# Two-layer graph network: the first layer norm on ScalarE, the own-feature products made ahead, and row chunk 0's own tiles kept for hop 1

## The chip, the cores and the metric

The kernel runs on one core of a Trainium2 chip. A core has five engines that work side by side, each through its own list of instructions in order: TensorE (PE in the profile) multiplies matrices into PSUM; VectorE (DVE), ScalarE (ACT) and GpSimd (POOL) do element-wise work; SyncE (SP) here only issues DMAs. ScalarE can issue DMAs too, between its other instructions. All DMAs run on sixteen DMA engines. Engines wait for each other through semaphores. The metric is the device time of one execution in microseconds (us); lower is better.

## What is computed

There are 4096 nodes with 64 features each and a sparse 4096 x 4096 matrix `adj` (64 MB in fp32). Layer 0 normalises the features, clips them at zero, and makes two hops; each hop multiplies by `adj`, puts the product beside the features it came from, and multiplies by a 128 x 64 weight. Layer 1 normalises again and sums neighbours with weights that are powers of a half, by the neighbour's rank in its row.

```python
h = relu(layernorm(x))
for k in range(2):                       # two hops
    agg = adj @ h
    h = tanh(concatenate([agg, h], axis=1) @ W[k])
x = x + h
h = relu(layernorm(x))
support = h @ weight
rank = cumsum(adj != 0, axis=1)
deg = rank[:, -1:]
k = minimum(deg, 100.)
pos = rank - (deg - k)
w = (adj != 0) * where(pos > 0, 0.5 ** (k - pos), 0.0)
x = x + (w @ support + bias)
```

`concatenate([agg, h]) @ W[k]` is two products added: the aggregate with the upper half of `W[k]`, and the node's own features with the lower half. The second is called the own-feature product here.

## The kernel before, in words

**Tiles.** `adj` is cut into four row chunks I = 0..3 of 1024 rows and 32 column blocks b of 128 columns. Transposed, one tile (I, b) is 128 x 1024 fp32, 512 KB. A feature tensor is held as 32 blocks of 128 nodes: `hx[:, b, :64]` holds the normalised features, `hx[:, b, 64:]` the result of hop 0. One matmul multiplies 64 or 128 columns of `hx` (the weights of TensorE) with 512 columns of a tile.

**Sweep 1** (`sweep1`) goes through the row chunks in order and, in each, through sixteen pairs of column blocks from b = 31 down to 0. For a pair n it issues the two loads on SP, then `count_pair` on DVE (five instructions that make the running count of non-zeros and store it as bytes in `codes`), then the matmuls of hop 0, then one `step()`, which carries a queue of small jobs written as generators on by one `yield`. A pair whose blocks lie in a row chunk that is already finished is *fused*: its matmul takes all 128 columns of `hx`, so that hop 1 is done for that tile in the same pass (L317). The other tiles (L211) get hop 0 alone and are loaded a second time in sweep 2.

**Buffers.** The pairs rotate through `ring` (three pairs) and, for I < 3, through the part of `codes` that belongs to row chunk 3 (four pairs more), so seven pairs can be loaded ahead. A pair's slot comes free when both DVE has counted it and TensorE has multiplied it.

**The first layer norm** (`ln_relu`) runs in row chunk 0, a chunk of eight blocks at a time: chunk 3 before the second pair, chunks 2, 1 and 0 as small jobs put in at n = 1, 5 and 9. Each has four wide instructions and one small one on DVE, a square on ACT, and a power of -0.5 on POOL (L157). The pairs n = 4q to 4q + 3 need chunk 3 - q. `load_x` and `load_weights` issue the loads of x and of the weights on SP, the weights between the first pair's loads and the second's.

**Finishing a row chunk.** `features_T` (at n = 12 of each row) transposes the chunk's own features into `hT`. `finish_row` then copies the sums out (`S`, `F`, and `tot`, the row counts, which waits for the last count), multiplies them and `hT` by the weights into `po`, takes the tanh (`x1T`), transposes it back into `hx[:, :, 64:]`, keeps hop 1's own part in `pre1`, and turns `tot` into `base` on DVE from the PSUM tile `pb`. Its parts are spread over the first pairs of the next row.

**Sweep 2** (`sweep2`) loads the tiles that were not fused again for hop 1, in the order of `parts`, and puts layer 1 between: `decode` turns codes into powers of two (ACT and DVE, L406, L398, L401), `add_base` adds `base` on DVE (L416), `layer1` multiplies. `share` says how many units of layer 1 go with each pair of tiles.

Of the kernel before, what the change touches and what calls it, by code (L numbers as in the profile page):

```python
# [7 lines left out]
F32 = mybir.dt.float32  # L8
# [8 lines left out]
P = 128  # L17
# [14 lines left out]
def gnn_kernel(  # L32
# [63 lines left out]
    def tmp(shape=None, dtype=F32, name="tmp"):  # L96
        return tpool.tile(shape or [P, C], dtype, tag="tmp", name=name)
# [4 lines left out]
    def two(name="two"):  # L102
        return pone.tile([P, C], F32, tag="two", name=name)


    def load_x(q):
        nc.sync.dma_start(pre1[:, chunk(q), :], xv[:, chunk(q), :])

# [5 lines left out]
    def load_weights():  # L114
        for h in range(2):
            rows = slice(h * D, (h + 1) * D)
            for k in range(HOPS):
                nc.sync.dma_start(wz[rows, h, k], W[k].rearrange("(h d) e -> d h e", h=2))
            nc.sync.dma_start(wa[rows], weight)

    warm = spool.tile([P, 1], F32, tag="warm", name="warm")
    nc.vector.memset(warm, 0.0)
# [20 lines left out]


    def ln_relu(dst, src, scale=1.0):
        wide = lambda ap: ap[:, :, None].to_broadcast([P, CB, D])
        s1 = spool.tile([P, CB], F32, tag="s1", name="s1")
        s2 = spool.tile([P, CB], F32, tag="s2", name="s2")
        xc = tmp([P, CB, D], name="xc")
        sq = tmp([P, CB, D], name="sq")  # L150
        nc.vector.tensor_reduce(s1, src, axis=AX.X, op=ALU.add)
        nc.vector.scalar_tensor_tensor(xc, wide(s1), -1.0 / D, src, op0=ALU.mult, op1=ALU.add)
        nc.scalar.activation(sq, xc, AF.Square)
        yield
        nc.vector.tensor_reduce(s2, sq, axis=AX.X, op=ALU.add)
        nc.vector.tensor_scalar(s2, s2, 1.0 / D, EPS, op0=ALU.mult, op1=ALU.add)  # L156
        nc.gpsimd.tensor_tensor(s2, s2, half, op=ALU.pow)  # L157
# [4 lines left out]
        nc.vector.scalar_tensor_tensor(dst, xc, 0.0, wide(s2), op0=ALU.max, op1=ALU.mult)  # L162
        return dst


    by_t = lambda ap: ap.rearrange("q (p t) -> q t p", t=TC)
# [70 lines left out]
        nc.scalar.copy(by_t(hT), pt.rearrange("q (t p) -> q t p", t=TC))  # L237
        return hT

    def finish_row(I, acc, hT):  # L240
        S = tmp(name="S")
        nc.scalar.copy(S, acc[:, NC, :])
        if I:
            F = [tmp(name="F") for _ in range(NC)]
            for c in range(NC):
                nc.scalar.copy(F[c], acc[:, c, :])
        tot = tmp([P, CW], BF16, name="tot")
        nc.scalar.copy(
            tot.rearrange("p (k m) -> p k m", k=2),
            cnts[I % 2].bitcast(U8).rearrange("p (m k) -> p k m", k=2),  # L250
        )
        yield
        po = one(name="po")
        terms = [(lambda c: wz[:, c, 0, 1], lambda c: hT), (lambda c: wz[:, c, 0, 0], lambda c: S)]
        if I:
            terms.append((lambda c: wz[:, 0, 0, 0], lambda c: F[c]))
        paired(po, terms)
        terms = [(lambda c: wz[:, 1, 1, 0], lambda c: F[c])] if I else []
        po1 = two(name="po1")
        if I:  # L260
            for c in range(NC):
                nc.tensor.matmul(
                    po1[c * D : (c + 1) * D, :], wz[:, 1, 1, 0], F[c], start=True, stop=False
                )
        x1T = tmp(name="x1T")
        nc.scalar.activation(x1T, po, AF.Tanh)
        yield
        pt = nodes(x1T)
        for c in range(NC):
            nc.tensor.matmul(  # L270
                po1[c * D : (c + 1) * D, :], wz[:, c, 1, 1], x1T, start=I == 0, stop=True
            )
        nc.scalar.copy(as_nodes(hx[:, chunk(I), D:]), pt)
        nc.scalar.copy(flat(pre1[:, chunk(I), :]), po1)
        yield
        for c in range(NC):
            pb = (one if c else two)(name="pb")
            nc.tensor.matmul(pb, tri, tot[:, c * C : (c + 1) * C], start=True, stop=True)
            nc.vector.tensor_scalar(
                base[:, I * CW + c * C : I * CW + (c + 1) * C], pb,  # L280
                off, -32768.0, op0=ALU.add, op1=ALU.max,
            )

    def sweep1():
        seq = 0
        first = ln_relu(hx[:, chunk(NCH - 1), :D], pre1[:, chunk(NCH - 1), :])
        load_x(NCH - 1)
        for I in range(NCH):
            acc = pacc.tile([P, 3, C], F32, tag="acc", name="acc")
            slots = [ring[:, s : s + 2, :] for s in range(0, RING, 2)]  # L290
            if I < NCH - 1:
                slots += [ring2[:, s : s + 2, :] for s in range(0, ring2.shape[1], 2)]
            for n, b in enumerate(range(NB - 1, 0, -2)):
                a = slots[seq % len(slots)]
                seq += 1
                for r in range(2):
                    nc.sync.dma_start(a[:, r, :], adjA[I, b - r])
                if I == 0:
                    if n == 0:
                        load_weights()  # L300
                        next(first)
                    elif n == 1:
                        for q in range(NCH - 2, -1, -1):
                            load_x(q)
                count_pair(I, b, a)
                if I == 0:
                    if n == 0:
                        for _ in first:
                            pass
                    if n % 4 == 1 and n < 12:  # L310
                        q = NCH - 2 - n // 4
                        steps.append(ln_relu(hx[:, chunk(q), :D], pre1[:, chunk(q), :]))
                for r in range(2):
                    g = b - r
                    if fused(I, g):
                        for c in range(NC):
                            nc.tensor.matmul(  # L317
                                acc[:, c, :], hx[:, g, :], a[:, r, c * C : (c + 1) * C],
                                start=g == CB * I - 1, stop=g == 0,
                            )  # L320
                    else:
                        agg_pair(acc[:, NC, :], hx[:, g, :D], a[:, r], g == NB - 1, g == CB * I)
                step()
                if n == 12:
                    hT = features_T(I)
            steps.append(finish_row(I, acc, hT))
            step()


# [176 lines left out]
    def sweep2():  # L506
        n_ring = 4
        early = pacc.tile([P, 3, C], F32, tag="acc", name="acc1")
        accs = {2: early[:, 0, :], 3: early[:, 1, :]}
        parts = [(2, 16, 24), (3, 24, 32), (2, 24, 32), (1, 8, 32), (0, 0, 32)]  # L510

        share = [0, 0, 0, 16 / 12, 22 / 16]
        owed = 0.0
        seq = 0
        space(ring[:, 4, :].bitcast(I16).rearrange("p (r k m) -> p r k m", r=2, k=2))
        space(ring[:, 5, :].bitcast(I16).rearrange("p (r k m) -> p r k m", r=2, k=2))
        for i, (I, b0, b1) in enumerate(parts):
# [63 lines left out]
```

## Time and profile before

| what | value |
|---|---|
| median of 3 runs | 478.34 us (475.04 to 479.42) |
| the profiled execution | 472.14 us, its span 470.1 us, 4623 instructions |
| busy in the span | PE 390.2 us, DVE 325.9 us, ACT 124.0 us, POOL 24.4 us |
| mean granted clock of TensorE | 0.956 |
| moved by DMA | 112.72 MB, mean 240 GB/s |

The profile is of one execution. A page gives busy times by engine, the span in forty slices, the DMA queues, the chain of work that ended last (followed back from the last instruction to what released it), and groups of instructions by source line. A group's row reads: line, engine, operation, output<-inputs, shape, xcount | busy us, mean ns of one | idle time of the engine just before, and what ended it. TensorE works an fp32 matmul in two passes, each with a record of its own, so a count of records is twice the count of matmuls; records of the two column halves overlap. By stages the span reads: sweep 1's row chunk 0 until about 64 us, row chunk 1 until 110, row chunks 2 and 3 until 211, sweep 2 until about 392, and the rest of layer 1 until 470.

### The profile page before, as it was taken

How to read it: one execution, taken by the hardware profiler on the slowest of the kernel's cores; microseconds unless marked ns; L12 is line 12 of the kernel's file. 1: busy time of each engine (PE TensorE's matmuls, PEld its weight loads, DVE VectorE, ACT ScalarE, POOL GpSimd, SP SyncE). 2: the span in 40 equal slices, each digit the busy share in tenths (PEclk: the TensorE clock that was granted, in tenths of full speed). 3: DMA queues.
4: the chain of work that ended last, by engine and by line, in shares of the span. 5: the costliest groups of instructions: out<-in, count | busy, mean ns of one | idle time of the engine just before them, and what ended most of it. 6: DMA issues, size and time to landing. Idle time of an engine off the chain costs nothing.

```text
span 470.1 us, 4623 instructions
## 1 busy us (share of the span) xinstructions
PE 390.2 (83%) x1632; PEld 147.1 (31%) x1632; DVE 325.9 (69%) x548; ACT 124.0 (26%) x150; POOL 24.4 (5%) x17
## 2 busy tenths in 40 slices
PE   0766599999999999996867958789879998953995
PEld 0211243344344434442212412223323333311342
DVE  4799998999999779750104564444688998997332
ACT  1000020012000300004001325353476775582000
POOL 0212200000000000000002030000110000200000
PEclk9997899999999999999999888899899999977999
DMA  7999999999987488837899654566457880000011
GB/s 213 371 410 408 410 401 366 379 388 393 348 313 261 162 282 316 299 117 270 312 337 322 227 180 162 196 229 241 160 199 252 279 293 5 1 1 0 1 45 45
DMA packets 32742, 112.72 MB, mean 240 GB/s; under 512 B 4560, under 2 KB 4560, under 8 KB 32720
## 3 DMA queue, kind: packets, MB, share of 16 engines
q1 hardware_dynamic: 32720, 112.44, 66.4%
q8 instruction: 12, 0.20, 0.2%
q14 instruction: 10, 0.08, 0.1%
HBM read 111.38 MB, written 1.05 MB: 239 GB/s over the span
## 4 chain that ended last, share of the span: by engine, by line
PE 53%; DVE 28%; DMA 9%; ACT 4%; issue 3%; POOL 2%; SPq 1%; ACTq 0%; POOLq 0%; DVEq 0%
PE acc L317 15%; PE acc L211 15%; PE accl L448 9%; DMA ring<-in_adjA_dram 9%; DVE m L194 5%; DVE ring L416 5%; PE accl L457 5%; DVE codes L204 4%; DVE codes L416 3%; PE pt L181 3%; PE po L172 2%; DVE codes L471 2%; ACT ring L406 2%; DVE lo L205 2%; POOL s L157 2%
## 5 line engine op out<-in xcount | busy, mean ns | idle before, releaser
L211 PE MATMUL acc<-ring,hx 128*64 128x512 f32 x472 | 118.5, 627 | 33.3 <-DVE hx L162 21.2
L211 PEld LDWEIGHTS acc<-ring,hx 128*64 128x64 f32 x472 | 33.2, 145 | 99.0 <-issue 41.2
L317 PE MATMUL acc<-ring,hx 128*128 128x512 f32 x144 | 63.0, 595 | 0.0
L416 DVE TENSOR_TENSOR ring<-ring,base 128x2048 uint16<-128x2048 int16 x34 | 41.1, 1219 | 29.3 <-ACT ring L406 29.3
L448 PE MATMUL accl<-ring,hx 128*128 128x512 bf16 x136 | 38.7, 412 | 25.4 <-DVE ring L416 18.3
L204 DVE TENSOR_TENSOR codes<-m,lo 128x512 uint16<-128x512 uint16 x124 | 52.8, 426 | 4.2
L194 DVE TENSOR_SCALAR m<-ring 128x2048 uint8<-128x2048 f32 x37 | 45.2, 1221 | 5.4 <-DMA ring<-in_adjA_dram 5.4
L448 PEld LDWEIGHTS <-hx 128*128 128x128 bf16 x256 | 23.5, 102 | 81.1 <-issue 47.2
L406 ACT ACTIVATE ring<-codes 128x1024 int16<-128x1024 uint8 x44 | 43.6, 1047 | 17.8 <-PE accl L457 17.8
L211 PE MATMUL acc<-codes,hx 128*64 128x512 f32 x168 | 39.9, 614 | 7.4 <-DVE hx L162 7.4
L406 ACT ACTIVATE codes<-codes 128x1024 int16<-128x1024 uint8 x42 | 40.7, 1042 | 12.0 <-PE accl L457 12.0
L205 DVE TENSOR_SCALAR lo<-codes 128x512 uint16<-128x512 uint16 x128 | 37.6, 294 | 4.5
L317 PEld LDWEIGHTS acc<-ring,hx 128*128 128x128 f32 x144 | 27.0, 190 | 34.5 <-issue 34.5
L157 POOL TENSOR_TENSOR s<-s,half 128x8 f32<-128x8 f32 x8 | 17.1, 2141 | 386.9 <-DVE s L156 386.9
L416 DVE TENSOR_TENSOR codes<-codes,base 128x2048 uint16<-128x2048 int16 x30 | 35.5, 1217 | 0.8 <-ACT codes L406 0.8
L448 PE MATMUL accl<-codes,hx 128*128 128x512 bf16 x120 | 30.3, 389 | 5.1 <-ACT codes L406 5.1
L194 DVE TENSOR_SCALAR m<-codes 128x2048 uint8<-128x2048 f32 x27 | 33.0, 1221 | 0.0
L237 ACT COPY hT<-ph 128x512 f32<-128x512 f32 x4 | 4.4, 1106 | 97.1 <-PE ph L232 97.1
L457 PE MATMUL accl<-ring,lo 128*64 128x512 bf16 x136 | 22.2, 428 | 0.0
L211 PEld LDWEIGHTS acc<-codes,hx 128*64 128x64 f32 x168 | 11.9, 141 | 32.2 <-issue 21.3
L317 PE MATMUL acc<-codes,hx 128*128 128x512 f32 x48 | 21.3, 597 | 0.0
L471 DVE TENSOR_TENSOR codes<-accl,codes 128x512 f32<-128x512 f32 x24 | 15.1, 683 | 7.2 <-PE accl L457 7.2
(74 smaller groups left out, 254.1 us busy)
## 6 DMA issues: line engine op xcount, KB each, us to landing
ring<-in_adjA_dram SPq DMA_DIRECT2D x154, 512.0 KB, 4.7
codes<-in_adjA_dram SPq DMA_DIRECT2D x54, 512.0 KB, 6.1
pre<-in_x_dram SPq DMA_DIRECT2D x4, 256.0 KB, 6.3
xres<-in_x_dram SPq DMA_DIRECT2D x4, 256.0 KB, 5.3
out_dram<-o SPq DMA_DIRECT2D x4, 256.0 KB, 2.5
wz<-in_W_dram SPq DMA_DIRECT2D x4, 32.0 KB, 5.4
wa<-in_weight_dram SPq DMA_DIRECT2D x2, 16.0 KB, 4.6
wz<-in_weight_dram SPq DMA_DIRECT2D x2, 16.0 KB, 4.4
```

The source lines that it names most:

```text
L157: nc.gpsimd.tensor_tensor(s2, s2, half, op=ALU.pow)
L181: nc.tensor.matmul(pt[:, t * P : (t + 1) * P], by_t(src)[:, t, :], ident, start=True, stop=True, skip_group_check=True,)
L194: nc.vector.tensor_scalar(m, a, 0.0, float(FLAG - 1), op0=ALU.not_equal, op1=ALU.mult)
L204: nc.vector.tensor_tensor(q, m[:, r].bitcast(U16), cnt, op=ALU.add)
L205: nc.vector.tensor_scalar(cnt, q, 0x7F7F, None, op0=ALU.bitwise_and)
L211: nc.tensor.matmul(acc[c * D : (c + 1) * D, :], src, a[:, c * C : (c + 1) * C], start=first, stop=last,)
L317: nc.tensor.matmul(acc[:, c, :], hx[:, g, :], a[:, r, c * C : (c + 1) * C], start=g == CB * I - 1, stop=g == 0,)
L406: nc.scalar.activation(w[:, r], src[:, r].rearrange("p (m k) -> p k m", k=2), AF.Copy, scale=float(FLAG))
L416: nc.vector.tensor_tensor(w.bitcast(U16), w, base[:, None, g * CW : (g + 1) * CW].to_broadcast([P, 2, CW]), op=ALU.add)
L448: nc.tensor.matmul(accs[-1][:, c, :], hm[:, CB * J + 2 * k + r, : 2 * D], w[:, r, c, :], start=k == 0 and r == 0, stop=k == CB // 2 - 1 an ...
L457: nc.tensor.matmul(acc[c * D : (c + 1) * D, 2, :], lo[:, CB * J + 2 * k + r, :], w[:, r, c, :], start=k == 0 and r == 0, stop=k == CB // 2 ...
L471: nc.vector.tensor_tensor(p, acc[:, q, :], p, op=ALU.add)
```

## The change

It has five parts, all in sweep 1 and in what sweep 2 takes over from it.

1. **Loads.** SP loads only two blocks of x (30 and 31) before the first pair; the other x loads and all weight loads are issued on ScalarE.
2. **Layer norm.** `ln_relu` is used for blocks 30 and 31 alone and finished before the first count. All other blocks use the new `ln_relu_blocks`: for each block two activations with a sum as second output (mean, then sum of squares), three POOL instructions on 128 x 8 values for the whole chunk, and one activation a block for the result.
3. **Own-feature products.** The new `own_share` makes the transposed features and their product with the lower half of `W[0]` for all four row chunks during row chunk 0 and keeps it in `pre1`; `finish_row` adds it on DVE ahead of the tanh.
4. **Kept tiles.** The last four pairs of row chunk 0 (blocks 7 to 0, the chunk's own columns) stay in their slots until the chunk's hop 0 is finished; hop 1 is then made from them, in a new part of `finish_row` (`agg_pair` over `held`), and `base` comes one part later.
5. **Sweep 2.** The part for row chunk 0 starts at block 8 rather than 0: eight loads and their matmuls fewer; its share of layer 1 is 22 units in 12 pairs rather than in 16.

```diff
-    def load_x(q):
-        nc.sync.dma_start(pre1[:, chunk(q), :], xv[:, chunk(q), :])
+    def load_x(engine, b0, b1):
+        engine.dma_start(pre1[:, b0:b1, :], xv[:, b0:b1, :])
...
-                nc.sync.dma_start(wz[rows, h, k], W[k].rearrange("(h d) e -> d h e", h=2))
-            nc.sync.dma_start(wa[rows], weight)
+                nc.scalar.dma_start(wz[rows, h, k], W[k].rearrange("(h d) e -> d h e", h=2))
+            nc.scalar.dma_start(wa[rows], weight)
...
+    def ln_relu_blocks(b0, b1):
+
+        nb = b1 - b0
+        m = spool.tile([P, CB], F32, tag="m", name="m")
+        s = spool.tile([P, CB], F32, tag="s", name="s")
+        junk = tmp([P, D], name="junk")
+        col = lambda ap, i: ap[:, i : i + 1]
+        for i in range(nb):
+            nc.scalar.activation(
+                junk, pre1[:, b0 + i, :], AF.Copy, scale=-1.0 / D, accum_out=col(m, i)
+            )
+            nc.scalar.activation(
+                junk, pre1[:, b0 + i, :], AF.Square, bias=col(m, i), accum_out=col(s, i)
+            )
+        s, m = s[:, :nb], m[:, :nb]
+        nc.gpsimd.tensor_scalar(s, s, 1.0 / D, EPS, op0=ALU.mult, op1=ALU.add)
+        nc.gpsimd.tensor_tensor(s, s, half[:, :nb], op=ALU.pow)
+        nc.gpsimd.tensor_tensor(m, m, s, op=ALU.mult)
+        yield
+        for i in range(nb):
+            nc.scalar.activation(
+                hx[:, b0 + i, :D], pre1[:, b0 + i, :], AF.Relu, scale=col(s, i), bias=col(m, i)
+            )
...
+    def own_share(I):
+
+        hT = features_T(I)
+        yield
+        po = two(name="po0")
+        paired(po, [(lambda c: wz[:, c, 0, 1], lambda c: hT)])
+        nc.scalar.copy(flat(pre1[:, chunk(I), :]), po)
+
...
-        terms = [(lambda c: wz[:, c, 0, 1], lambda c: hT), (lambda c: wz[:, c, 0, 0], lambda c: S)]
+        terms = [(lambda c: wz[:, c, 0, 0], lambda c: S)]
...
-        nc.scalar.activation(x1T, po, AF.Tanh)
+        nc.vector.tensor_add(x1T, po, flat(pre1[:, chunk(I), :]))
+        nc.scalar.activation(x1T, x1T, AF.Tanh)
...
         nc.scalar.copy(as_nodes(hx[:, chunk(I), D:]), pt)
+        yield
+        if I == 0:
+
+            for n, (b, a) in enumerate(held):
+                agg_pair(acc[:, 0, :], hx[:, b, D:], a, n == 0, n == len(held) - 1)
+            G = tmp(name="G")
+            nc.scalar.copy(G, acc[:, 0, :])
+            yield
+            for c in range(NC):
+                nc.tensor.matmul(
+                    po1[c * D : (c + 1) * D, :], wz[:, c, 1, 0], G, start=False, stop=True
+                )
         nc.scalar.copy(flat(pre1[:, chunk(I), :]), po1)
...
+                if I == 0 and n == 0:
+                    load_x(nc.scalar, NB - CB, b0)
+                    for _ in first:
+                        pass
+                    for q in range(NCH - 2, -1, -1):
+                        load_x(nc.scalar, q * CB, q * CB + CB)
+                    load_weights()
+                    for _ in ln_relu_blocks(NB - CB, b0):
+                        pass
+                if I == 0 and n % 4 == 1 and n < 12:
+                    q = NCH - 2 - n // 4
+                    steps.append(ln_relu_blocks(q * CB, q * CB + CB))
+                if I == 0 and n in (2, 6, 10, 13):
+                    steps.append(own_share(NCH - 1 - n // 4))
                 count_pair(I, b, a)
...
+                    if I == 0 and g < CB:
+                        held.append((g, a[:, r]))
                 step()
-                if n == 12:
-                    hT = features_T(I)
-            steps.append(finish_row(I, acc, hT))
+            steps.append(finish_row(I, acc, held))
...
-        parts = [(2, 16, 24), (3, 24, 32), (2, 24, 32), (1, 8, 32), (0, 0, 32)]
-
-        share = [0, 0, 0, 16 / 12, 22 / 16]
+        parts = [(2, 16, 24), (3, 24, 32), (2, 24, 32), (1, 8, 32), (0, 8, 32)]
+
+        share = [0, 0, 0, 16 / 12, 22 / 12]
...
-                agg_pair(acc, hx[:, b, D:], a, b == CB * I, b == NB - 1)
+                agg_pair(acc, hx[:, b, D:], a, b == max(CB * I, CB), b == NB - 1)
```

More of the change, by code (lines that the diff above doesn't have):

```diff
@@ L145, in ln_relu @@
     def ln_relu(dst, src, scale=1.0):
[L146 to L150, printed above, removed]
+        nb = src.shape[1]
+        wide = lambda ap: ap[:, :, None].to_broadcast([P, nb, D])
+        s1 = spool.tile([P, CB], F32, tag="s1", name="s1")[:, :nb]
+        s2 = spool.tile([P, CB], F32, tag="s2", name="s2")[:, :nb]
+        xc = tmp([P, CB, D], name="xc")[:, :nb]
+        sq = tmp([P, CB, D], name="sq")[:, :nb]
         nc.vector.tensor_reduce(s1, src, axis=AX.X, op=ALU.add)
@@ L156, in ln_relu @@
         nc.vector.tensor_scalar(s2, s2, 1.0 / D, EPS, op0=ALU.mult, op1=ALU.add)
-        nc.gpsimd.tensor_tensor(s2, s2, half, op=ALU.pow)
+        nc.gpsimd.tensor_tensor(s2, s2, half[:, :nb], op=ALU.pow)
         yield
@@ L238, in features_T, with finish_row @@
         return hT
-    def finish_row(I, acc, hT):
+    def own_share(I):
[4 more added lines that the diff above has]
+        nc.scalar.copy(flat(pre1[:, chunk(I), :]), po)
+    def finish_row(I, acc, held):
         S = tmp(name="S")
@@ L257, in finish_row @@
         paired(po, terms)
-        terms = [(lambda c: wz[:, 1, 1, 0], lambda c: F[c])] if I else []
         po1 = two(name="po1")
@@ L270, in finish_row @@
             nc.tensor.matmul(
-                po1[c * D : (c + 1) * D, :], wz[:, c, 1, 1], x1T, start=I == 0, stop=True
+                po1[c * D : (c + 1) * D, :], wz[:, c, 1, 1], x1T, start=I == 0, stop=I > 0
             )
         nc.scalar.copy(as_nodes(hx[:, chunk(I), D:]), pt)
+        yield
[9 more added lines that the diff above has]
+                )
         nc.scalar.copy(flat(pre1[:, chunk(I), :]), po1)
@@ L285, in sweep1 @@
         seq = 0
-        first = ln_relu(hx[:, chunk(NCH - 1), :D], pre1[:, chunk(NCH - 1), :])
-        load_x(NCH - 1)
+        b0 = NB - 2
+        load_x(nc.sync, b0, NB)
+        first = ln_relu(hx[:, b0:, :D], pre1[:, b0:, :])
+        held = []
         for I in range(NCH):
@@ L297, in sweep1 @@
                     nc.sync.dma_start(a[:, r, :], adjA[I, b - r])
[L298 to L304, printed above, removed]
-                count_pair(I, b, a)
[L306 to L312, printed above, removed]
+                if I == 0 and n == 0:
[12 more added lines that the diff above has]
+                    steps.append(own_share(NCH - 1 - n // 4))
+                count_pair(I, b, a)
                 for r in range(2):
```

## The prediction

> **What bounds the kernel now.** I read the span by stages first: busy time of each engine in three stretches (columns: stretch, length, then PE, PEld, DVE, ACT, POOL busy with instruction counts, granted clock, DMA share, GB/s).
>
> ```profile
> 14.40:64.40 50.00, 35.77 (x152) 11.62 (x154) 47.05 (x92) 3.59 (x5) 7.89 (x3) 0.90 1.02 407
> 64.40:110.00 45.60, 45.60 (x188) 17.74 (x186) 42.48 (x83) 5.50 (x9) 0.00 (x0) 1.00 1.00 383
> 110.00:211.00 101.00, 100.67 (x322) 43.07 (x318) 86.01 (x166) 9.17 (x13) 0.00 (x0) 1.00 0.76 273
> ```
>
> Row chunk 0 is paced by DVE (47 of 50 us busy) with the DMA engines full beside it (407 GB/s), while ACT works 3.6 us. Row chunk 1 is paced by DVE too: counting a pair takes 1.22 + 2 x (0.43 + 0.29) us plus gaps, 2.71 us from pair to pair in the timeline, and 16 x 2.71 = 43.4. Row chunks 2 and 3 are TensorE's (100.67 of 101.00). Next the timeline of row chunk 0, to see whom TensorE waits for:
>
> ```profile
> 22.66 2.68 POOL L157 TENSOR_TENSOR s<-s,half 128x8 f32<-128x8 f32 x1 [8.91 <-DVE s L156]
> ...
> 25.37 0.69 DVE L162 SCALAR_TENSOR_TENSOR hx<-xc,s 128x512 f32<-128x512 f32 x1
> ...
> 26.12 5.37 PE L211 MATMUL acc<-codes,hx 128*64 128x512 f32 x24 [2.29 <-DVE hx L162]
> ...
> 39.85 5.14 PE L211 MATMUL acc<-ring,hx 128*64 128x512 f32 x16 [6.65 <-DVE hx L162]
> ...
> 53.59 3.39 PE L211 MATMUL acc<-codes,hx 128*64 128x512 f32 x8 [5.15 <-DVE hx L162]
> ```
>
> The number in brackets is idle time and what ended it. TensorE needs 1.72 us for a pair (eight records, two side by side every 0.43 us) and is early each time; the chunk of normalised features releases it, at 26.1, 39.9 and 53.6, 13.8 us apart. The copy of the finished sum shows when row 0 is done on TensorE, and the rows of ACT and POOL give prices:
>
> ```profile
> 63.11 0.58 ACT L242 COPY S<-acc 128x512 f32<-128x512 f32 x1 [4.09 <-PE acc L211]
> ```
>
> ```profile
> L153 ACT ACTIVATE sq<-xc 128x512 f32<-128x512 f32 x8 | 5.0, 630 | 56.1 <-DVE xc L152 56.1
> ...
> L237 ACT COPY hT<-ph 128x512 f32<-128x512 f32 x4 | 4.4, 1106 | 97.1 <-PE ph L232 97.1
> ...
> L123 ACT ACTIVATE warm<-warm 128x1 f32<-128x1 f32 x1 | 0.2, 203 | 0.0
> ```
>
> So row 0 ends on TensorE at E = 63.0 us; row 1 is paced by DVE until 110; then nothing but TensorE's work counts until 211. An end of row 0 that comes later or earlier is passed on whole.
>
> **What the Trainium skill says.** *ScalarE: Activation LUTs*, What ACT_TABLE_LOAD costs: an ACTIVATE takes 186 ns + 0.833 ns an element with immediate scale and bias, 93 ns more for each per-partition pointer operand, and back-to-back ones overlap by 93 ns. The trace is near: 203 ns for one element, 630 for 512 (613 to 706 by the page). *SBUF — State Buffer*, Who interferes with whom: a DVE instruction with two SBUF inputs contends with a POOL instruction that reads SBUF. The trace agrees: L157 takes 1.65 us where DVE is waiting for it (12.10 us) and 2.61 to 2.68 beside counting. *VectorE: DVE Perf Modes*, Two Vector instructions with no wait between them: an operation that also writes its accumulator is two instructions; it says so of Vector, and no page prices it on ScalarE. *DMA: Bandwidth & Descriptors*, Issuing engines are not separate DMA queues: issuing from another engine saves only issue time. With 407 GB/s from SP alone, ACT's loads cannot add rate.
>
> **The change, part by part.** DVE is relieved: three chunks x (0.68 + 0.69 + 0.68 + 0.17 + 0.69) = 8.7 us, and 2 more at the start. Counting alone, from about 8 us, would be done at 8 + 43.4 = 51.4 instead of 64.4. But TensorE now waits for a chain over ACT and POOL, which I add up.
>
> *Start on ACT.* Ten DMAs move onto ACT's queue (SP's rows: 0.43 an x load, 0.7 a weight load). In the order of the changed kernel DMAs take eight completion semaphores in turn, and a DMA that reuses one waits until the earlier DMA on it has landed. So the last weight load waits on ACT for the first half of pair 3. Ahead of that stand 1.05 MB of x and seven halves, 4.7 MB; at 407 GB/s 11.6 us, after about 2 us to the first bytes, plus its own 0.7: A = 14.3 us. Behind it, in order, stands the first statistic. Bounds 11 to 17. SP gains the weight loads' 4.2 us, which nothing waits for any more.
>
> *One chunk on ACT.* Per block: Copy with a sum 0.24 us, Square with pointer bias 0.33 (the page's prices at 64 elements), each waiting for the one before (0.04 twice). The sum's read-out has no row: zero if it is free, 0.20 if it is an instruction like the 203 ns one; I take half, 0.10 twice. Total 0.85 a block, bounds 0.5 and 1.1; eight blocks 6.8, six 5.1. POOL: the power 2.65, and two small instructions that the trace does not show, between the 0.1 of a memset and the 1.3 of L363 on 128x512; I take 0.35 each and 0.15 for hand-overs: 3.5, bounds 2.5 and 5. Nothing on ACT can go ahead meanwhile. Results: 0.425 with two pointers less the overlap, 0.33 a block: 2.7 for eight, 2.0 for six.
>
> *Own products in the same queue.* Behind the results stand the copy hT (1.1), then the product on TensorE (four records, 0.86, and hand-overs: 1.0), then its copy (0.6 + 0.1), and only then the next chunk's first statistic. They are no extra work for ACT, but they are in the loop: 6.8 + 3.5 + 2.7 + 1.1 + 1.0 + 0.7 = 15.8 us per chunk, against 13.8 before.
>
> *End of row 0.* Six blocks: 14.3 + 5.1 + 3.5 + 2.0 = 24.9. Two loops: 56.5. Last chunk with its product: 15.1, 71.6. Then pairs 12 and 13 (3.4), the transposes (0.9), pair 14 (1.7), the product (0.9), pair 15 (1.7): E = 80.2, **17.2 us later**. Slots hold DVE back meanwhile, so that its relief is lost.
>
> *Row 1.* Four of seven pair slots stay held until hop 1. From E: pair 0 of row 1 and `po` 2.6; the new add on DVE 0.7 and tanh 0.6, pair 1, transposes and product until E + 7.4; pair 2; hop 1 is sixteen matmuls, 6.9, from E + 9.1. The first slot is released at E + 10.9, and a ring load lands 4.7 us after issue (the median): DVE, out of tiles, resumes at E + 15.5, counts two pairs, waits for `pb`, and has 11 x 2.71 left after E + 22.4: row 1 counted at E + 52.2. The add for row 1 stands behind one more count on DVE (2.7) and ahead of tanh, so TensorE's transposes begin at E + 56.3; before, 111.58 - 63.0 = 48.6. **Cost 7.7**; bounds 3 and 10.
>
> *Rows 2 and 3.* TensorE loses two sets of transposes (1.02 each) and one product (0.86): **-2.9**. The add hides behind a pair's 1.72 us there, since DVE is ahead.
>
> *Sweep 2.* Four pairs x 1.72 = 6.9 us of TensorE go. Around them DVE becomes the limit: from 345 to 390 it is busy 39.1 of 45 us and waits about 5 for TensorE. **-5**, bounds 0 and -8. The 4.2 MB fewer loads count nothing: no wait for DMA stands in that part.
>
> Sum: 17.2 + 7.7 - 2.9 - 5.0 = +17.0 us. On the profiled execution 472.14 + 17.0 = 489.1; that execution lies 6.2 below the median, to which I add it: 478.34 + 17.0 = 495.3.
>
> **The rivals.** *Faster: DVE's relief is what counts.* For it: DVE and DMA are the busy ones, ACT has 46 idle us in row 0. If the ACT loop were about 9 us, E would be DVE's 51.4 + 2.6 = 54, 9 us earlier: -9.0 + 7.7 - 2.9 - 5.0 = -9.2, 469 us. It decides below E = 63.2, a loop of about 11.4; 1% faster needs about 10. Against it: sixteen small instructions and one power alone give over 7.
> *Even: the low prices hold.* No read-out, 0.5 a block, POOL 2.5, results 0.27 a block: loop 11.5, E = 14.3 + 7.1 + 23 + 10.8 + 8.6 = 63.8, total +0.6: 479.
> *Dearer: every read-out 0.2 and POOL 4.2.* Loop 18.3, E about 90, total +27: 505.
> *The held slots do not stall* (loads land sooner): the forecast less 5, 490, inside its own range.
>
> **How the numbers follow.** Forecast 0.60, its own range 484 to 503; dearer 0.16; even 0.13; faster 0.11. The range 477 to 509 leaves out faster and a part of the even and dearer cases. About 1% (4.8 us) is what a measurement can tell from no change, the runs of before spreading 0.9%. Faster 0.11, within 1% 0.13, slower 0.76.
>
> **What would show it.** Right: TensorE idle in row 0 released by ACT's results, about 16 us apart; the row-0 sum copied near 80; ACT's first statistic near 14; a DVE wait for ring DMA of several us after hop 1. Wrong: the row-0 sum copied before 63, statistics under 0.55 a block, or DVE busy nine tenths up to 50 us.

## The result and the profile after

| | before | after |
|---|---|---|
| median on the same chip | 476.69 us (475.01 to 479.42) | 520.05 us (518.25 to 521.87) |
| ratio | | 1.0904, 95% interval [1.0825, 1.0983] |
| span of the profiled execution | 470.1 us | 516.5 us |
| mean granted clock of TensorE | 0.956 | 0.917 |
| moved by DMA | 112.72 MB | 108.55 MB |

The kernel became 9% slower: the direction was forecast, the size was not (495 forecast, range 477 to 509). Some executions of a kernel fall into a slower state, over 1.5% above its fastest; the ratios here leave them out, the medians do not. I cut both spans at marks that the trace shows in both kernels: the copy `S` of row 0's sum on ACT, and the first transpose (`pt`) on TensorE of the tanh of row 1, of row 3, and of the last two row chunks of sweep 2. Each column is the time from the mark before; the forecast is that of the prediction.

| us | to row 0's copy | to `pt` of row 1 | to `pt` of row 3 | to `pt`, second last of sweep 2 | to `pt`, last | to the end |
|---|---|---|---|---|---|---|
| before | 63.1 | 48.5 | 110.7 | 107.7 | 67.8 | 72.3 |
| after | 89.1 | 58.9 | 105.9 | 107.7 | 72.6 | 82.2 |
| difference | +26.0 | +10.4 | -4.8 | 0 | +4.8 | +9.9 |
| forecast | +17.2 | +7.7 | -2.9 | -5.0 from here on | | |

The differences add up to 46.3 of the 46.4 us. Each column is read from one execution. The fourth, where the code is all but the same in every kernel here, lies between 106 and 112 us in the experiments below, so that a difference of several us in it, or in the third, need not come from the code; the last two repeat within 1.5 us where the code there is the same. The busy time by stretch, for after (same columns as before: stretch, length, busy time of PE, PEld, DVE, ACT, POOL with counts, granted clock, DMA share, GB/s):

```profile
17.80:89.00 71.20, 42.13 (x202) 15.01 (x204) 37.03 (x71) 40.22 (x158) 13.45 (x12) 0.74 0.60 221
89.00:141.90 52.90, 49.38 (x186) 16.60 (x182) 41.26 (x79) 3.93 (x6) 0.00 (x0) 1.00 0.81 315
141.90:245.00 103.10, 102.32 (x309) 43.12 (x308) 86.40 (x166) 9.32 (x16) 0.00 (x0) 1.00 0.81 301
```

In row 0 no engine is full any more: TensorE, DVE and ACT are each busy for about half of it, the sign of one chain that passes through all of them, and the DMA engines fell from 407 to 221 GB/s. The timeline of ACT in row 0, which answers to the waits of TensorE shown of before:

```profile
17.86 0.26 ACT L174 ACTIVATE junk<-pre 128x64 f32<-128x64 f32 x1 [13.40 <-DMA wa<-in_weight_dram]
18.02 0.19 ACT L174 ACTIVATION_READ_ACCUMULATOR junk<-pre 128x1 f32 x1
18.24 0.35 ACT L177 ACTIVATE junk<-pre,m 128x64 f32<-128x64 f32 x1
18.50 0.19 ACT L177 ACTIVATION_READ_ACCUMULATOR junk<-pre,m 128x1 f32 x1
...
55.43 2.77 ACT L186 ACTIVATE hx<-pre,m,s 128x64 f32<-128x64 f32 x8 [3.99 <-POOL m L183]
58.10 1.06 ACT L262 COPY hT<-ph 128x512 f32<-128x512 f32 x1
61.24 0.59 ACT L271 COPY pre<-po 128x512 f32<-128x512 f32 x1 [2.08 <-PE po L197]
...
89.09 0.59 ACT L275 COPY S<-acc 128x512 f32<-128x512 f32 x1 [1.07 <-PE acc L236]
```

This is the loop of the prediction: statistics, a wait of 3.99 us for POOL, eight results, the copy `hT`, a wait of 2.08 us for the product, its copy, and only then the next chunk's first statistic. The copies of the products come at 44.12, 61.24 and 78.42: a loop is 17.1 to 17.2 us. TensorE shows the same loop from its side, and what it does to its pace:

```profile
42.08 1.97 PE L197 MATMUL po<-hT,wz 128*64 128x512 f32 x4 [4.27 <-ACT hT L262]
59.21 1.98 PE L197 MATMUL po<-hT,wz 128*64 128x512 f32 x4 [6.96 <-ACT hT L262]
...
76.41 1.97 PE L197 MATMUL po<-hT,wz 128*64 128x512 f32 x4 [7.05 <-ACT hT L262]
78.17 5.71 PE L236 MATMUL acc<-codes,hx 128*64 128x512 f32 x16
...
86.30 1.02 PE L197 MATMUL po<-hT,wz 128*64 128x512 f32 x4
```

The same four records take 1.97 us after an idle time of 4 to 7 us and 1.02 at 86.30, when TensorE has been busy for 8 us. The Trainium skill, *TensorE: Matmul & The Clock Gate*, Part 1, says that the array runs at half clock after some 3.4 us without work; the trace agrees, 1.97 against 1.02, with a granted clock of 0.50 from 76 to 80 us and 1.00 from 84 to 88.

Row 1 on DVE:

```profile
91.74 0.69 DVE L298 TENSOR_TENSOR x1T<-po,pre 128x512 f32<-128x512 f32 x1 [18.07 <-PE po L197]
92.35 1.22 DVE L219 TENSOR_SCALAR m<-codes 128x2048 uint8<-128x2048 f32 x1
...
95.06 1.22 DVE L219 TENSOR_SCALAR m<-codes 128x2048 uint8<-128x2048 f32 x1
...
104.70 1.23 DVE L219 TENSOR_SCALAR m<-codes 128x2048 uint8<-128x2048 f32 x1 [6.85 <-DMA codes<-in_adjA_dram]
```

DVE sat idle for 18 us at the end of row 0: its relief was lost. It waited there for `po`, not for tiles: the new add stands in DVE's list ahead of row 1's second pair, and it needs the sum of row 0. Two more pairs lay loaded (the DMA engines moved next to nothing from 76 to 100 us), and DVE counted them right after the add, at 92.35 and 95.06. Then it did wait for a load and resumed at 104.70, 15.6 us after the copy, where the prediction had 15.5. The held slots set that restart, so the wait for the add should have cost nothing more in this kernel; that was not tried.

### The profile page after: what moved, and what is told of

Its sections match the earlier page's. It is cut to its first block, busy times and chain, and to the rows that moved or that the text cites. A ratio compares the mean times of both kernels' runs of the same rounds, so it can differ in the third digit from the quotient of the medians.

```text
span 516.5 us, 4747 instructions
## 1 busy us (share of the span) xinstructions
PE 402.2 (78%) x1636; PEld 149.7 (29%) x1636; DVE 320.2 (62%) x537; ACT 158.4 (31%) x302; POOL 29.0 (6%) x26
## 2 busy tenths in 40 slices
DMA packets 31736, 108.55 MB, mean 210 GB/s; under 512 B 4448, under 2 KB 4704, under 8 KB 31712
## 4 chain that ended last, share of the span: by engine, by line
PE 52%; DVE 18%; DMA 13%; ACT 11%; POOL 3%; issue 2%; SPq 0%; ACTq 0%; DVEq 0%
PE acc L364 16%; PE acc L236 14%; DMA ring<-in_adjA_dram 9%; PE accl L495 8%; DVE ring L463 5%; PE accl L504 5%; DVE codes L463 4%; PE po L197 3%; DMA codes<-in_adjA_dram 3%; DVE codes L518 3%; ACT junk L177 3%; PE pt L206 2%; ACT junk L174 2%; ACT hx L186 2%; ACT ring L453 2%
## 5 line engine op out<-in xcount | busy, mean ns | idle before, releaser
L219 DVE TENSOR_SCALAR m<-ring 128x2048 uint8<-128x2048 f32 x37 | 45.2, 1222 | 17.1 <-DMA ring<-in_adjA_dram 17.1
L463 DVE TENSOR_TENSOR ring<-ring,base 128x2048 uint16<-128x2048 int16 x35 | 42.4, 1222 | 18.1 <-ACT ring L453 18.0
L236 PE MATMUL acc<-codes,hx 128*64 128x512 f32 x184 | 46.1, 628 | 1.6 <-DMA codes<-in_adjA_dram 1.6
L495 PE MATMUL accl<-codes,hx 128*128 128x512 bf16 x116 | 31.5, 410 | 9.2 <-DVE codes L463 9.1
L275 ACT COPY S<-acc 128x512 f32<-128x512 f32 x4 | 2.3, 587 | 117.5 <-PE acc L364 116.5
L158 POOL TENSOR_TENSOR s<-s,half 128x8 f32<-128x8 f32 (+1 forms) x5 | 9.1, 1821 | 366.0 <-DVE s L157 366.0
L504 PE MATMUL accl<-ring,lo 128*64 128x512 bf16 x140 | 24.4, 459 | 0.0
L236 PEld LDWEIGHTS acc<-codes,hx 128*64 128x64 f32 x184 | 13.0, 145 | 32.8 <-issue 23.9
L298 DVE TENSOR_TENSOR x1T<-po,pre 128x512 f32<-128x512 f32 x4 | 2.8, 692 | 31.9 <-PE po L197 31.9
```

The costliest lines, as they stand in the source:

```text
L219: nc.vector.tensor_scalar(m, a, 0.0, float(FLAG - 1), op0=ALU.not_equal, op1=ALU.mult)
L236: nc.tensor.matmul(acc[c * D : (c + 1) * D, :], src, a[:, c * C : (c + 1) * C], start=first, stop=last,)
L463: nc.vector.tensor_tensor(w.bitcast(U16), w, base[:, None, g * CW : (g + 1) * CW].to_broadcast([P, 2, CW]), op=ALU.add)
L495: nc.tensor.matmul(accs[-1][:, c, :], hm[:, CB * J + 2 * k + r, : 2 * D], w[:, r, c, :], start=k == 0 and r == 0, stop=k == CB // 2 - 1 an ...
L504: nc.tensor.matmul(acc[c * D : (c + 1) * D, 2, :], lo[:, CB * J + 2 * k + r, :], w[:, r, c, :], start=k == 0 and r == 0, stop=k == CB // 2 ...
```

## What the end of sweep 2 shows

No step of the prediction had anything there but a gain, and 14.7 us were lost. First the group of layer 1's matmuls on ring tiles, of before and then of after:

```profile
L448 PE MATMUL accl<-ring,hx 128*128 128x512 bf16 x136 | 38.7, 412 | 25.4 <-DVE ring L416 18.3
```

```profile
L495 PE MATMUL accl<-ring,hx 128*128 128x512 bf16 x140 | 39.2, 408 | 39.5 <-DVE ring L463 27.6
```

TensorE waits for converted tiles (`add_base` on DVE) 9.3 us more. Then the timeline of TensorE after the last tanh, where layer 1 is all that is left (before, then after):

```profile
432.26 1.89 PE L448 MATMUL accl<-ring,hx 128*128 128x512 bf16 x4 [7.12 <-DVE codes L471]
```

```profile
478.64 1.89 PE L495 MATMUL accl<-ring,hx 128*128 128x512 bf16 x4 [11.88 <-DVE codes L518]
```

The code says why conversions can be late. While the tiles are loaded again, each pair of tiles is followed by `decode(2)`, at most two conversions, and by its share of `layer1`. Before, the last part had 16 pairs: 16 x 2 = 32 conversions at most against 22 units that TensorE used up, so that the lead could grow by 10. Now it has 12 pairs and the share is still 22: 12 x 2 = 24, the lead can grow by 2, TensorE has to wait for DVE, and conversions that could have been made beside it are left to the end. That was a theory from the code and these waits; the experiments below test it.

## Experiments

Each is an edit on the kernel after (`-` and `+` against it) unless it says otherwise. Ratios are to the kernel before on the same chip.

**1. More conversions in the last part.**

```diff
                         owed -= layer1(int(owed))
-                    decode(2)
+                    decode(3 if i == 4 else 2)
```

> The changed kernel with decode(3) instead of decode(2) in the last part of sweep 2 alone. Theory 'the decode cap': 12 steps of at most two units make just the 24 units that layer 1 takes there, so that no lead builds up, TensorE waits for DVE in each step, and free spaces are filled only at the end. Then the stretch from the second-last tanh of sweep 2 to the end (154.8 us in the changed kernel, 140.0 before) falls to 135 to 142, and the time to 503 to 508. Rival 'DVE is simply full there': the same DVE work, only earlier, 517 to 521.

Measured: 502.09 us, ratio 1.0587 [1.0527, 1.0647]. The last two columns are 67.0 and 71.6, together 138.6 against 154.8 (before 140.0). The group of the matmuls waits as before again:

```profile
L495 PE MATMUL accl<-ring,hx 128*128 128x512 bf16 x131 | 37.1, 401 | 25.0 <-DVE ring L463 17.9 <-DVE codes L518 6.6 <-DVE lo L409 0.2
```

So the cap on conversions is the cause of the loss at the end, all of it. And with it lifted, four pairs of matmuls fewer are worth 1.4 us, not 5 (1.6 in experiment 6).

Rows 0 to 3 are the same code here as in the kernel after, yet row 0 took 85.3, not 89.1 (84.9 and 86.0 in experiments 2 and 7, whose row 0 is the same up to its last pairs). So some 4 us of the 26.0 belong to that one execution. Where they arise shows in ACT's waits for POOL ahead of the eight results: 2.32 to 4.49 us over these four executions, 3.05, 3.99 and 4.08 in the one shown; why they vary was not tested.

**2. No pair kept; sweep 2's last part from block 0 again, 22 units in 16 pairs.** The hop 1 of the kept pairs goes out of `finish_row` with it.

```diff
...
-                    if I == 0 and g < CB:
+                    if I == 0 and g < 0:
...
-        parts = [(2, 16, 24), (3, 24, 32), (2, 24, 32), (1, 8, 32), (0, 8, 32)]
+        parts = [(2, 16, 24), (3, 24, 32), (2, 24, 32), (1, 8, 32), (0, 0, 32)]
...
-        share = [0, 0, 0, 16 / 12, 22 / 12]
+        share = [0, 0, 0, 16 / 12, 22 / 16]
```

> The changed kernel without kept tiles: no hop 1 from them, the last part of sweep 2 from block 0 with 22 units in 16 pairs, as before; layer norm, loads and own-feature products as changed. Theory: row chunk 0 still ends on TensorE at 88 to 90 us (26 later than before), the row chunk 1 stretch (48.5 us before, 58.9 in the changed kernel, from the copy of the row-0 sum to the transposes of row 1) falls back to 46 to 50, the last stretch to 140; time 496 to 501. Rival 'the held slots cost nothing, row 1 is long for the new add alone': the row 1 stretch stays above 55, time 505 or more.

Measured: 493.44 us, ratio 1.0411 [1.0346, 1.0475]. Row 1 takes 49.3 (58.9 with kept pairs), the last two columns 67.8 and 72.4. Keeping the pairs cost 9.6 us in row 1 and, by the cap, 14.6 at the end. DVE's wait of 6.85 us for a load after hop 1 is gone, which confirms the held slots. Its wait for the new add is still 14.23 us here; whether an add placed later would pay was not tried.

**3. All layer norms on DVE as before (`ln_relu` for the six blocks and for chunks 2 to 0), the weight loads on SP; kept pairs, own products and the x loads on ScalarE as in the kernel after.**

```diff
...
-                steps.append(ln_relu_blocks(q * CB, q * CB + CB))
+                steps.append(ln_relu(hx[:, chunk(q), :D], pre1[:, chunk(q), :]))
...
-                nc.scalar.dma_start(wz[rows, h, k], W[k].rearrange("(h d) e -> d h e", h=2))
+                nc.sync.dma_start(wz[rows, h, k], W[k].rearrange("(h d) e -> d h e", h=2))
```

> The changed kernel with the wide DVE layer norm for all chunks (blocks 24 to 29 around the first count, chunks 2 to 0 at n = 1, 5, 9), weights loaded from SP after the second pair; own products and kept tiles as changed. Theory 'the chain over ScalarE makes row chunk 0 late': the row-0 sum is copied at 61 to 65 us instead of 89, everything after shifts with it, time 493 to 498. Rival 'own products and their waits make it late': the copy stays above 75, time over 507.

Measured: 500.55 us, ratio 1.0542 [1.0465, 1.0620].

```profile
65.02 0.59 ACT L275 COPY S<-acc 128x512 f32<-128x512 f32 x1 [1.19 <-PE acc L236]
```

Row 0 ends at 65.0: with the norms on DVE the loss of row 0 is gone but for 2 us, though all four own products are still made there. Row 1 (59.5) and the end (73.8 and 82.3) keep theirs. The time is above the 493 to 498 expected; the third and fourth columns are 3.4 and 3.1 us longer than in the kernel after, within what other executions show.

**4. Only the weight loads back on SP**, after the second pair's loads.

```diff
-                nc.scalar.dma_start(wz[rows, h, k], W[k].rearrange("(h d) e -> d h e", h=2))
-            nc.scalar.dma_start(wa[rows], weight)
+                nc.sync.dma_start(wz[rows, h, k], W[k].rearrange("(h d) e -> d h e", h=2))
+            nc.sync.dma_start(wa[rows], weight)
...
-                    load_weights()
...
+                if I == 0 and n == 1:
+                    load_weights()
```

> The changed kernel with the weight loads back on SP, behind the second pair's loads; the loads of x stay on ScalarE. Theory: the first statistic stands behind the DMA issues on ScalarE's queue (17.9 us in the changed kernel); without the six weight loads it starts at 10 to 12.5 and the row-0 sum is copied 5 to 8 us earlier, time 512 to 515. Rival: the chunk loop absorbs it, the copy stays at 87 to 90 and the time at 518 to 521.

Measured: 513.04 us, ratio 1.0839 [1.0775, 1.0904].

```profile
12.65 0.26 ACT L174 ACTIVATE junk<-pre 128x64 f32<-128x64 f32 x1 [8.00 <-DMA pre<-in_x_dram]
```

The first statistic starts 5.2 us earlier, and row 0 ends at 81.35. Of the 7.7 us by which that is earlier, 5.2 are the wait at the start; the other 2.5 lie within the scatter of row 0.

**5. The own products of all chunks put behind the last norm** (at n = 11), out of the loop of the norms; nothing else changed.

```diff
-                if I == 0 and n in (2, 6, 10, 13):
-                    steps.append(own_share(NCH - 1 - n // 4))
+                if I == 0 and n == 11:
+                    steps.extend(own_share(q) for q in range(NCH - 1, -1, -1))
```

> The changed kernel with all four own-feature products put at n = 11 and after, so that they no longer stand between one chunk's results and the next chunk's statistics on ScalarE. Theory: the loop from statistics to statistics falls from 17.1 to about 13.6 us, twice, the row-0 sum is copied at 80 to 84 us, time 6 to 8 us below the changed kernel. Rival 'the loop is set by POOL and the statistics alone': the copy stays at 87 to 90.

Measured: 512.00 us, ratio 1.0804 [1.0715, 1.0893]; row 0 ends at 80.80. The chunks' results start 13.0 and 12.0 us apart, after 17.1 and 17.2. The products' place between the chunks cost 8.3 us against this profile of the kernel after, 4.5 against the 85.3 of experiment 1.

**6. DVE norms and `decode(3)` together** (experiments 1 and 3).

> The changed kernel with both mendings together: layer norm on DVE (weights on SP) and decode(3) in the last part of sweep 2; kept tiles and own-feature products as changed. Theory: the three costs are in series and add up, so that the time lies 12 to 17 us below the run with DVE's layer norm alone: 1.01 to 1.03 of before. Rival: the lead that decode(3) builds was already lost to an earlier wait, less than 6 us.

Measured: 481.27 us, ratio 1.0096 [1.0067, 1.0125]. Taken away together, the two causes give back what they gave alone: row 0 24.6 us (24.1 in experiment 3) and the end 16.4 (16.3 in experiment 1). The median is 19.3 us below that of experiment 3, more than the 12 to 17 expected; in the profiles the end alone gives 17.7. What is left is row 1 (58.4 against 48.5), less small gains in rows 2 and 3 and at the end.

**7. Two pairs kept instead of four.**

```diff
-                    if I == 0 and g < CB:
+                    if I == 0 and g < 4:
...
-        parts = [(2, 16, 24), (3, 24, 32), (2, 24, 32), (1, 8, 32), (0, 8, 32)]
+        parts = [(2, 16, 24), (3, 24, 32), (2, 24, 32), (1, 8, 32), (0, 4, 32)]
...
-        share = [0, 0, 0, 16 / 12, 22 / 12]
+        share = [0, 0, 0, 16 / 12, 22 / 14]
```

> The changed kernel with two pairs kept (blocks 3 to 0) instead of four; the last part of sweep 2 from block 4, 22 units in 14 pairs. Theory: five free slots are enough to carry DVE to hop 1's release, so the row 1 stretch (58.9 us; 49.3 with nothing kept) falls to 51 to 54; with 28 units decoded against 22 taken a lead builds up, and the stretch from the second-last tanh to the end falls from 154.8 to 140 to 148. Rival 'hop 1 itself, not the held slots, lengthens row 1': half of hop 1, so 54 to 56, in proportion.

Measured: 500.91 us, ratio 1.0548 [1.0494, 1.0603]. Row 1 53.0, the last two columns 65.1 and 78.0. Both costs follow the number of kept pairs. At the end, the lead can grow by 2, 6 and 10 units with four, two and no kept pairs, and the two columns together are 154.8, 143.1 and 140.2.

**8. DVE norms, weights on SP and no pair kept:** of the change only the own products in row 0 with their add on DVE, the x loads on ScalarE and the first norm in two steps (two blocks and six) are left.

> All first-layer norms on DVE as in the kernel before, weights on SP, no pair kept for hop 1; of the change only the own-feature products made in row 0 and the first norm of two blocks with the six blocks after it are left. If the costs found so far add up, row 0 is as in the two versions with DVE norms (65), row 1 as in the version without kept pairs (49.3), rows 2 and 3 107 to 109, sweep 2 as before (107.7, 67.8, 72.3): span 469 to 473, ratio 0.995 to 1.01. If the own-feature products in row 0 still cost something by themselves where no ScalarE loop is, row 0 is 67 or more and the ratio above 1.01.

Measured: 473.14 us, ratio 0.9956 [0.9924, 0.9988]; row 0 ends at 63.1, the span is 470.6. The own products made early cost nothing that this can tell where no ScalarE loop runs: DVE paces the row and TensorE has room. The whole slowdown is thus placed: norms and weight loads on ScalarE, kept slots, and the cap.

**9. A mixture, to save DVE work without a chain:** no pair kept, weights on SP, chunk 2 on DVE, only chunks 1 and 0 by `ln_relu_blocks`, issued well before they are needed (beside the edits of experiment 8):

```diff
-                    for q in range(NCH - 2, -1, -1):
+                    for q in (1, 2, 0):
...
+                    late = [ln_relu_blocks(q * CB, q * CB + CB) for q in (1, 0)]
+                    next(late[0])
...
+                if I == 0 and n == 1:
+                    steps.append(ln_relu(hx[:, chunk(2), :D], pre1[:, chunk(2), :]))
+                if I == 0 and n == 2:
+                    next(late[1])
+                if I == 0 and n in (3, 5):
+                    for _ in late[n // 4]:
+                        pass
+                if I == 0 and n in (4, 7, 10, 13):
+                    steps.append(own_share({4: 3, 7: 2, 10: 1, 13: 0}[n]))
```

> A version meant to beat both: no kept tiles; layer norm of chunks 3 and 2 on DVE, of chunks 1 and 0 on ScalarE with their statistics started early (before the second and third pair) and their results well ahead of need; own-feature products made ahead at n = 4, 7, 10, 13; weights from SP after the second pair. Theory: ScalarE's chain hurts only by standing in line just ahead of its use; with a start that is early enough it takes 6 us of layer norm off DVE, so the row-0 sum is copied at 56 to 61 us (63 before, 89 in the changed kernel), rows 2 and 3 keep their 3 to 4 us of gain, the rest is as before: 6 to 10 us faster than before. Rival 'small ScalarE instructions are too slow in any order': the copy at 66 or later, no faster than before.

Measured: 486.80 us, ratio 1.0234 [1.0166, 1.0303]; row 0 ends at 72.85. A miss; the timeline of POOL and DVE shows why:

```profile
22.91 0.20 POOL L181 TENSOR_SCALAR s<-s 128x8 f32<-128x8 f32 x1 [17.17 <-ACT junk L177]
23.19 1.64 POOL L182 TENSOR_TENSOR s<-s,half 128x8 f32<-128x8 f32 x1
24.91 0.20 POOL L183 TENSOR_TENSOR m<-m,s 128x8 f32<-128x8 f32 x1
25.07 1.32 POOL L158 TENSOR_TENSOR s<-s,half 128x6 f32<-128x6 f32 x1
...
26.42 0.56 DVE L163 SCALAR_TENSOR_TENSOR hx<-xc,s 128x384 f32<-128x384 f32 x1 [14.95 <-POOL s L158]
```

POOL works its list in order. Its instruction for chunk 1, which is needed at pair 8, stood ahead of the power for blocks 24 to 29, which are needed at once, and waited until 22.91 for ScalarE's statistics; DVE waited 14.95 us behind it.

**10. The mixture with POOL's order mended:** chunk 1's statistics are issued after chunk 2's power, chunk 0's two pairs later, and x is loaded for chunk 2 ahead of chunk 1 again (against experiment 9).

```diff
-                    for q in (1, 2, 0):
+                    for q in (2, 1, 0):
...
-                    next(late[0])
...
-                if I == 0 and n == 2:
-                    next(late[1])
-                if I == 0 and n in (3, 5):
-                    for _ in late[n // 4]:
+                if I == 0 and n in (3, 5):
+                    next(late[n // 4])
+                if I == 0 and n in (4, 6):
+                    for _ in late[n // 6]:
                         pass
```

> As the mixed version before it (weights back on SP, no pair kept for hop 1, only chunks 1 and 0 normalised on ScalarE, chunk 2 and the rest of chunk 3 on DVE), but written so that nothing that waits for ScalarE stands on GpSimd's queue ahead of a power that DVE needs soon: chunk 1's statistics are issued after chunk 2's power, chunk 0's two pairs after that. If GpSimd's order was what made the mixed version miss (DVE waited 14.95 us at 26.42 and 5.04 us at 42.27 for a power), those two waits are gone, DVE is saved two normalisations (5.8 us) against the kernel before, and the row-0 sum is copied at 56 to 61 us instead of 72.85; with rows 1 to 3 and sweep 2 as in the mixed version the span is 464 to 470 (before 470.1), ratio 0.985 to 1.00. If instead the ScalarE chain or the own-feature products inside the row are what holds TensorE whatever the order, the copy stays at 66 or later and the span above 474.

Measured: 476.25 us, ratio 0.9962 [0.9922, 1.0002]; row 0 ends at 65.15. DVE's two long waits are gone (the longest for POOL is 1.44 us), so POOL's order was a cause, but the copy is later than the 56 to 61 expected. TensorE's timeline names the rest:

```profile
47.06 1.97 PE L197 MATMUL po<-hT,wz 128*64 128x512 f32 x4 [6.46 <-ACT hT L262]
```

The copy `hT` that this product needs stood on ACT's list behind the statistics and results of chunk 0. The same fault again, on another queue.

**11. Three own products later** (behind pairs 10, 12 and 14 instead of 7, 10 and 13, against experiment 10), so that their copies stand behind chunk 0's results.

```diff
-                if I == 0 and n in (4, 7, 10, 13):
-                    steps.append(own_share({4: 3, 7: 2, 10: 1, 13: 0}[n]))
+                if I == 0 and n in (4, 10, 12, 14):
+                    steps.append(own_share({4: 3, 10: 2, 12: 1, 14: 0}[n]))
```

> The mended mixed version with the last three sets of own-feature products put later, behind pairs 10, 12 and 14 instead of 7, 10 and 13, so that their copies stand on ScalarE's queue behind chunk 0's statistics and results and not ahead of the middle of them. In the mended version TensorE waited 6.46 us at 47.06 for a copy hT that stood behind chunk 0's statistics, and the row-0 sum was copied at 65.15. If that queue order was the rest of the miss, the wait is gone, the copy comes at 58 to 61, and the span is 463 to 467 (before 470.1, mended mixed 469.9), ratio 0.98 to 0.992. If what is saved in row 0 is given back in row 1 (DVE is then ahead of the loads, which the later rows need as before), the copy comes at 58 to 61 all the same but the span stays at 468 to 471, ratio 0.993 to 1.00. If the order was not the cause, the copy stays at 64 or later.

Measured: 468.02 us, ratio 0.9842 [0.9793, 0.989]: faster than both kernels, than the one before by 1.1 to 2.1%. Its row 0 by stretch, and its end:

```profile
20.00:59.00 39.00, 31.97 (x186) 12.67 (x188) 36.40 (x72) 22.88 (x83) 8.98 (x7) 0.96 1.03 410
```

```profile
59.65 0.59 ACT L275 COPY S<-acc 128x512 f32<-128x512 f32 x1
```

DVE is busy for 36.40 of 39.00 us and the DMA engines are full again (410 GB/s, after 221). Row 0 ends 3.5 us before that of the kernel before, of the 5.8 us that two norms less on DVE are worth at 2.9 each. The rest of the span's gain (463.9 against 470.1) is 4.2 in rows 2 and 3, where the own products are gone (1.4 to 5.2 in the other experiments), less 0.3 in row 1 and 1.2 in sweep 2.

## Why the prediction was wrong

The error is 29.4 us of span: 46.4 measured, 17.0 forecast. By its terms:

- **Row 0, 17.2 forecast, 26.0 measured.** The mechanism was right: TensorE waits for ACT's loop, 17 us apart where 16 was forecast, though three of its four long waits end with the copy `hT` and not with the results; and DVE's relief is lost. Three terms were too small. *A*, the start: 17.86 instead of 14.3, +3.6; the last weight load went out at 17.30, forecast 13.6. *The loop*: three rounds, up to the end of the last product, took 3.3 more. Of it the statistics are not the cause: eight blocks took 6.83, forecast 6.8: a read-out is a full 0.19, not the half of 0.20 that I took, but it overlaps its neighbours, so that a block recurs after 0.86 us. The product took 2.1 with hand-overs, forecast 1.0, since TensorE was at half pace after its idle time, and POOL's wait was 3.99 in the round shown, forecast 3.5. *The tail* from the end of that product to E: 10.6, forecast 8.6, the same half pace (16 records of pairs 12 and 13 took 5.71 us, forecast 3.4). Together 8.9; some 4 of these are the scatter that experiment 1 showed. The rival "dearer" had E about 90, but by a loop of 18.3 us (its terms add up to 18.1), where 17.1 to 17.2 was measured; that it comes near is luck. The prediction put DVE's lost relief down to slots alone; the last 18 us of it are the new add, which stands in DVE's list.
- **Row 1, 7.7 forecast, 10.4 measured.** Right as a mechanism, shown by experiments 2 and 7, and DVE's restart and the end of its counting (E + 52.2) to a tenth of a us. Mis-sized was the end on TensorE: TensorE was put at E + 56.3 and came at E + 58.9. Its matmuls of the blocks not fused were paced by loads, one each 1.28 us from 112.75 on, and the fused ones began only at 127.93, E + 38.8 (in experiment 2 at E + 25.1). The prediction had followed DVE there and not TensorE. Its reading of row 1 before, "paced by DVE too", was half of it: TensorE is busy for 45.60 of 45.60 us in the line that it shows, and waits only 0.34 us for DVE's last count at the end, so that a faster DVE alone could have gained next to nothing there.

```profile
112.75 1.08 PE L236 MATMUL acc<-ring,hx 128*64 128x512 f32 x4 [0.20 <-DMA ring<-in_adjA_dram]
114.02 1.08 PE L236 MATMUL acc<-ring,hx 128*64 128x512 f32 x4 [0.19 <-DMA ring<-in_adjA_dram]
```

- **Rows 2 and 3, -2.9 forecast, -4.8 measured.** Right in sign; the -2.9 is the transposes and product taken away. Other runs show -1.4 to -5.2 in this column against before, so the difference is not explained further.
- **Sweep 2, -5.0 forecast, +14.7 measured: the step that failed, two thirds of the error.** It counted the matmuls that go and took DVE's limit as a bound on the gain. It did not follow layer 1's share, which the change itself had raised per pair, through the conversions: 22 units in 12 pairs against a cap of two conversions a pair. The bounds "0 and -8" excluded a loss without a reason. Experiments 1, 6 and 7 show the cap; experiment 1 also sizes the true gain at 1.4. A likely reason, not tested apart, is that DVE has the same conversions to make whether or not TensorE's matmuls stand around them.
- **Own products.** In the forecast they were in the loop for 2.8 us a round; experiment 5 confirms that their place costs, and experiment 8 that their work does not.

With DVE norms row 0 ended at 65.0 and 64.5 where pairs were kept (experiments 3 and 6) and at 63.1 where none was (experiment 8); whether the kept pairs or scatter make that difference stays open.

## What to carry to other kernels

Work put on an engine that is nearly idle paid here only when its list held nothing that waits for another engine in front of something that is needed soon: from experiment 9 to experiment 11 the ratio fell from 1.0234 to 0.9842 with the same instructions in another order. Where a change makes a loop shorter, look for every quantity that is issued per step of that loop, and compare it with what is used up per step: here the saved loads took along the chances to convert. A buffer kept longer is paid for at the loads that wait for it, and here the restart could be worked out from the release, the time of a load and the work behind it.

## What the runs showed of the hardware

- The sum of an activation is read out by an instruction of its own on ScalarE, which takes 189 ns after the Copy and 188 after the Square; over the whole group:

```profile
L174 ACT ACTIVATION_READ_ACCUMULATOR junk<-pre 128x1 f32 x30 | 5.7, 189 | 0.0
```

- Small POOL instructions on 128 x 8 values took 0.20 us (L181, L183) and 1.64 (the power) in experiment 9, where DVE was idle, and 0.61, 0.57 and 2.24 in the mean of the kernel after. The prediction had 0.35, 0.35 and 2.65.
- Waits of 4.3 to 7.1 us cost TensorE twice in row 0 of the kernel after, once as idle time and again as half pace after it: 1.97 against 1.02 us for four records, and 5.71 for the next sixteen, against 3.60 at 87.16.
